# Loading the first image ahead of the small weights, touching two activation tables early, and spare matrix products at two places of a convolution-attention-recurrence kernel

## The chip, the cores and the metric

The kernel runs on one core of a Trainium2 chip. The metric is device time in microseconds: the median of three runs of the kernel before is 6977.31 us (6975.09 to 6978.62).

## What is computed

The input x has four images of 128 channels by 64 x 64 points, in float32. Each image goes through two layers, and the second ends in a recurrence that runs over all four together. Cut to what matters:

```
# layer 0: attention over 4096 points, after a normalisation over groups of 4 channels
xn    = (x - mean_g) / sqrt(var_g + 1e-5)             # needs the whole image first
e1,e2 = prelu(w1 @ xn + b1, a1), prelu(w2 @ xn + b2, a2)
asm   = prelu(wa @ xn + ba, aa)
x     = x + softmax(e1^T e2) applied to asm
# layer 1, per token (t = x transposed)
t = t + attention(layer_norm(t))                      # 16 heads of 8, queries = cos products;
                                                      # inside: zf = cos(.) * cos(ry); h = relu(zf @ w1.T + b1)
t = t + rnn(layer_norm(t)):                           # Wx = layer_norm(t) @ W.T, batch norm over all tokens
    y_t = sigmoid(Wx_t + y_{t-1} @ V.T)               # 4096 steps
```

## The kernel before, in words

**The order of the work.** The body first loads the weights and prepares them, then goes through the four images in a loop. For each image `first_stage` runs layer 0 (and, beside it, the feed-forward part of the image before), and `second_stage` runs the attention of layer 1. After the loop `last_stage` does the feed-forward part of the fourth image, and a last part (the stage named "runs") does the recurrence and writes the output. In these stages the order of TensorE's, ScalarE's and VectorE's instructions is written by hand: what stands earlier in the code is earlier in the engine's queue, and an engine whose next instruction waits does nothing behind it. The queues of SP and, outside the attention, of GpSimd are filled by a scheduler which knows only dependencies and the order of the code.

**The head.** The weights of layer 0 (w1, w2, b1, b2, wa, aa, a1, a2) are loaded by GpSimd (L152, L139, L162), all other weights by ScalarE's queue (L139, L200 to L207), and the first image by SP in four pieces of 512 KB (L1512). VectorE negates a1/a2, aa and b1/b2 (L167, L169), splits the rows of biases into a rounded part and a rest (L326 to L328), takes the statistics of the image in eight pieces of 512 columns (`norm_stats`: `bn_stats` at L350, the aggregate at L353, then two small products on TensorE at L357 and L366 that sum over channel groups, with the small operations L359 to L363 and L239 and a power on GpSimd at L241 between and after them). It also takes the cosine of `ry` (L246 to L253, the sine table on ScalarE at L255), scales a weight matrix by it, splits it (L317 to L320) and lets SP copy half of the rest part (L322). These preparing tiles lie in a pool named setup, which is closed before the images begin; its memory is used again by the image's tile q.

**Layer 0.** `layer0` begins with `first_pieces`: VectorE normalises 512 columns into q (L378), TensorE makes the convolutions (L391, L427, with the bias rows as a product with ones at L296), ScalarE applies the two halves of prelu (L398, L399, L337, L338), VectorE joins them (L410, L339) and splits e2 and e1 into rounded part and rest (L414, L415, L484, L485). Then for 8 blocks of 512 queries and 16 pairs of key tiles: two products per tile on TensorE (L503), exp on ScalarE (L507), the weighted sum on TensorE (L514), and the running total on VectorE (L528). Within each block `meanwhile` is called 16 times; it advances by one step the work per token of the block before (`tokens`: transposes, layer norm, cosines). A float32 product appears in the profile as two MATMUL instructions.

**The recurrence.** 4096 steps are run as 128 runs of 32 steps beside each other, each with 14 steps ahead of it from a guessed state (`WARM`), in two halves k of the images. Eight PSUM banks are first written by a product (L1790), then VectorE writes into each bank the scaled inputs of two steps (`seed`, L1808), TensorE adds the product with V (L1837), and ScalarE applies the sigmoid (L1842). From step 10 on VectorE also adds the results to the rows t2 (L1821), which are then stored (L1857). The last lines compare two states and decide on a slow exact way, which is not taken here.

Of the kernel before, what the change touches and what calls it, by code (L numbers as in the profile page):

```python
# [10 lines left out]
F32 = mybir.dt.float32  # L11
# [15 lines left out]
def kernel(  # L27
# [107 lines left out]
    loader = [nc.gpsimd]  # L135
# [9 lines left out]
    def load_both(one, two, name, axis):  # L145

        shape = list(one.shape)
        shape[axis] *= 2
        t = const.tile(shape, F32, tag=name, name=name)
        for i, ap in enumerate((one, two)):  # L150
            part = t[:, ts(i, CR)] if axis else t[ts(i, CR), :]
            nc.gpsimd.dma_start(out=part, in_=ap)  # L152
        return t
# [7 lines left out]
    for i, ap in enumerate((a1, a2)):  # L161
        nc.gpsimd.dma_start(out=a12_sb[ts(i, CR), :], in_=ap.partition_broadcast(CR))  # L162
# [3 lines left out]
    for t in (a12_sb, aa_sb):  # L166
        nc.vector.tensor_scalar(t, t, -1.0, None, ALU.mult)  # L167
    minus_b12 = const.tile([P, 1], F32, tag="minus_b12", name="minus_b12")
    nc.vector.tensor_scalar(minus_b12, b12_sb, -1.0, None, ALU.mult)  # L169
# [3 lines left out]
    for sign, base in ((1, 0), (-1, 3)):  # L173
# [10 lines left out]
    loader[0] = nc.scalar  # L184
    rx_bc = load_row(rx, "rx_bc")
    wc_sb = load(w_combT, "wc_sb")

    f1_sb = const.tile([P, NF, P], F32, tag="f1_sb", name="f1_sb")
    ry_sb = once.tile([P, 1], F32, tag="ry_sb", name="ry_sb")
    nc.gpsimd.memset(ry_sb, 0.0)  # L190
    setup = ctx.enter_context(ExitStack())
    setup_pool = setup.enter_context(tc.tile_pool(name="setup", bufs=1, reuse_waits="tile"))
    f1_all, f1_low = (
        setup_pool.tile([P, NF * P], F32, tag=name, name=name) for name in ("f1_all", "f1_low")
    )
    biases = setup_pool.tile([33, 4, P], F32, tag="biases", name="biases")
    nc.gpsimd.memset(f1_all, 0.0)
    for i in range(2):
        for k, ap in enumerate((ba, b_comb, fb2, be1)):
            nc.scalar.dma_start(out=biases[ds(32 * i, 1), k, :], in_=ap)  # L200
    for g in range(4):
        nc.scalar.dma_start(out=f1_all[ds(D * g, D), :], in_=f1T)
        nc.scalar.dma_start(out=ry_sb[ds(D * g, D), :], in_=ry)
    fb1_sb, f2_sb = load(fb1, "fb1_sb"), load(f2T, "f2_sb")
    g1_bc, be1_z = load_row(g1, "g1_bc"), const.tile([P, D], F32, tag="be1_z", name="be1_z")
    be1_bc = setup_pool.tile([P, P], F32, tag="be1_bc", name="be1_bc")
    nc.scalar.dma_start(out=be1_bc, in_=be1.partition_broadcast(P))  # L207
    g2_bc, be2_bc = load_row(g2, "g2_bc"), load_row(be2, "be2_bc")
    WT_sb, VT_sb = load(WT, "WT_sb"), load(VT, "VT_sb")
    gamma_sb, beta_sb = load(gamma, "gamma_sb"), load(beta, "beta_sb")  # L210


    nc.vector.tensor_copy(be1_z, be1_bc[:, 0:D])
# [98 lines left out]
    ck = once.tile([P, 1], F32, tag="ck", name="ck")  # L312
    cr = once.tile([P, 1], F32, tag="cr", name="cr")
    cry = once.tile([P, 1], F32, tag="cry", name="cry")
    for _ in cos_steps(cry, ry_sb, ck, cr):
        pass
    nc.vector.tensor_scalar(f1_all, f1_all, cry, None, ALU.mult)  # L317
    f1_high = f1_sb.rearrange("p f e -> p (f e)")
    nc.vector.tensor_copy(f1_high.bitcast(F32R), f1_all)
    nc.vector.tensor_tensor(f1_low, f1_all, f1_high, ALU.subtract)  # L320

    nc.sync.dma_start(out=f1_high[ds(2 * D, 2 * D), :], in_=f1_low[ds(2 * D, 2 * D), :])  # L322

    for row in (0, 32):
        at = slice(row, row + 1)
        nc.vector.tensor_tensor(biases[at, 2], biases[at, 2], biases[at, 3], ALU.add)  # L326
        nc.vector.tensor_copy(bias_rows[at].bitcast(F32R), biases[at, 0:3])
    nc.vector.tensor_tensor(  # L328
        bias_rows[at].bitcast(F32R), biases[at, 0:3], bias_rows[at], ALU.subtract
    )  # L330
    setup.close()


# [1174 lines left out]
    def load_x(n, rows):  # L1508

        xs = by_channel.tile([P, S], F32, tag="xs", name=f"xs{n}")  # L1510
        for i in range(4):
            nc.sync.dma_start(out=xs[:, ts(i, S // 4)], in_=x_rows[rows, ts(i, S // 4)])  # L1512
        return xs

# [54 lines left out]
    def first_stage(im, before):  # L1569
# [12 lines left out]
        with stage(f"conv{n}", {}, others, **pools, **psum), tc.manual_schedule(engines=engines):  # L1582
            own, calls = [], [0]
            step_late = in_steps(feed_forwards(before) if before else [], 13, 3)

            def meanwhile(steps=1):

                calls[0] += 1
                if before and calls[0] in (14, 17, 20):
                    before["left"].pop(0)()  # L1590
                for _ in range(steps):
                    step_first(own)

                for _ in range(0 if calls[0] <= 8 else 2 if calls[0] % 8 == 0 else 1):
                    step_late()

            norm = im["norm"] or list(norm_stats(n, im["xs"]))[-1]
# [129 lines left out]
    x_rows = x.rearrange("n c s -> (n c) s")  # L1727
    t2_rows = [t2_dram[ts(n, P), :] for n in range(N)]
    before = None
    x_next = {"xs": load_x(0, ts(0, P))}  # L1730
# [9 lines left out]
    for n in range(N):  # L1740
        image = open_image(n, ts(n, P), "right" if n % 2 else "left", **x_next)
        tail = first_stage(image, before)
# [22 lines left out]
    with stage("runs", t2=((P, 2 * IC), 4 * N), half=(HALF, 2 * NS + 2), ps_one=(ONE, NS * NB)):  # L1765
# [22 lines left out]
        for j in range(NB):  # L1788
            for k in range(NS):
# [7 lines left out]
                )  # L1797

# [27 lines left out]
        with tc.manual_schedule(  # L1826
            engines={nc.tensor.engine, nc.scalar.engine, nc.vector.engine}
        ):
            y = [None] * NS
# [164 lines left out]
```

## Time and profile before

| | us |
|---|---|
| median of three runs | 6977.31 |
| profiled execution, its own time | 6976.16 |
| its span in the trace | 6974.4 |
| first normalisation of the first image (L378) begins | 23.86 |
| first exp of layer 0 (L507) begins | 35.74 |
| first sigmoid (L1842) begins | 6884.95 |
| last instruction of VectorE (L1877) begins | 6960.72 |

The page of the profile gives, first, each engine's busy time. A view of groups gives, for a kind of instruction, how many there are, their mean time and what ended the idle time before them. The timeline gives instructions of one kind that follow each other as one line: start and length in us from the start of the span, engine, line of the code, operation, tile written and tiles read, shapes, how many, and in square brackets how long the engine stood idle before and for whom. ACTq and SPq are the queues in which ScalarE and SP issue DMAs; the length there is that of the issue, not of the transfer.

### The profile page before, as it was taken

The page shows a single profiled execution, that of the slowest core. Times are in us where ns is not written, and L with a number is a line of the kernel's source. Part 1 is how long each engine was busy: PE and PEld are TensorE (multiplying, and loading weights), DVE is VectorE, ACT ScalarE, POOL GpSimd, SP SyncE. Part 2 cuts the span into 40 slices and gives each one's busy share as a digit, 9 for nine tenths or more (in the row PEclk, how much of TensorE's full clock was granted, in tenths as well). Part 3 has the DMA queues.
Part 4 walks back from the last instruction along what each step waited for, and adds up shares of the span by engine and source line. Part 5 has one row for each costly group of instructions (what it writes and reads, how often), then busy time and mean ns, then how long its engine had stood idle before and what let it go on. Part 6 is the DMA issues. An engine that isn't in the chain of part 4 may idle for free. (4 is left out here: it accounts for less than half of the span.)

```text
span 6974.4 us, 223486 instructions
## 1 busy us (share of the span) xinstructions
PE 6808.2 (98%) x92333; PEld 3655.8 (52%) x92333; DVE 5966.9 (86%) x8064; ACT 5937.1 (85%) x11843; POOL 2795.6 (40%) x10008
## 2 busy tenths in 40 slices
PE   8999999999999999999999999999999999999997
PEld 4545555555664555555565455555456555555554
DVE  6688889897888898888787989898978898988887
ACT  4479999996669999999565999999956699999985
POOL 1134444444333444443433344444343344444442
PEclk9999999999999999999999999999999999999998
DMA  1110000000111000000011100000001100000012
GB/s 32 37 41 25 24 28 21 22 10 23 46 51 42 28 21 22 21 22 9 31 49 52 37 22 21 22 21 24 22 22 50 52 30 22 21 25 24 19 62 110
DMA packets 84760, 219.87 MB, mean 32 GB/s; under 512 B 9384, under 2 KB 10288, under 8 KB 82960
## 3 DMA queue, kind: packets, MB, share of 16 engines
q1 hardware_dynamic: 80448, 200.34, 8.5%
q8 instruction: 726, 11.89, 0.7%
q10 hardware_dynamic: 3024, 4.99, 0.2%
q14 instruction: 306, 2.51, 0.1%
q0 software_dynamic: 256, 0.13, 0.0%
HBM read 141.44 MB, written 56.62 MB: 28 GB/s over the span
## 5 line engine op out<-in xcount | busy, mean ns | idle before, releaser
L1069 ACT ACTIVATE e<-s 128x1024 f32<-128x1024 f32 (+1 forms) x3480 | 2952.7, 903 | 113.1 <-PE s L1057 82.8
L832 DVE STREAM_TRANSPOSE t<-e 128x1024 f32<-128x1024 f32 x2240 | 2594.0, 1210 | 75.7 <-ACT e L1069 73.0
L845 PEld LDWEIGHTS misc<-t,mirror 128*32 128x32 f32 x57344 | 1655.4, 110 | 1327.5 <-issue 1270.4
L845 PE MATMUL misc<-t,mirror 128*32 128x128 f32 x57344 | 1967.1, 273 | 18.7 <-DVE later L859 15.9
L1069 ACT ACTIVATE xs<-s 128x1024 f32<-128x1024 f32 (+1 forms) x2152 | 1840.7, 910 | 54.4 <-PE s L1057 42.6
L832 DVE STREAM_TRANSPOSE t<-xs 128x1024 f32<-128x1024 f32 x1344 | 1562.5, 1210 | 42.8 <-ACT xs L1069 41.3
L866 PE MATMUL acc<-e,q_aug 128*32 128x512 f32 x11360 | 1523.4, 608 | 1.1 <-POOL q_aug L748 1.1
L1057 PE MATMUL s<-queries,keys 32*128 32x512 f32 x9216 | 1245.9, 496 | 20.1 <-ACT e L1069 10.0
L912 POOL COPY own<-o 32x36 f32<-32x36 f32 x2048 | 430.4, 210 | 1802.5 <-DVE o L904 1722.6
L514 PE MATMUL acc<-p,asmT 128*128 128x512 f32 x2048 | 947.7, 594 | 1.6 <-DVE e L410 1.6
L866 PE MATMUL acc<-xs,q_aug 128*32 128x512 f32 x7072 | 942.2, 605 | 0.0
L507 ACT ACTIVATE p<-s 128x1024 f32<-128x1024 f32 x512 | 500.2, 1023 | 404.7 <-PE s L503 400.7
L1057 PEld LDWEIGHTS s<-queries,keys 32*128 32x128 f32 x9216 | 487.9, 182 | 602.1 <-issue 297.2
L937 POOL COPY other<-turned 32x64 f32<-32x64 f32 x1904 | 449.5, 236 | 622.4 <-DVE turned L927 543.9
L1069 ACT ACTIVATION_READ_ACCUMULATOR e<-s 128x1 f32 x2880 | 697.0, 242 | 0.0
L802 POOL COPY mirror<-q 32x128 f32<-32x128 f32 x2048 | 604.3, 295 | 198.5 <-PE misc L845 110.7
L503 PE MATMUL s<-hl,e 128*128 128x512 f32 x2048 | 587.7, 428 | 21.0 <-ACT hl L465 11.1
L528 DVE TENSOR_TENSOR total<-total,p 128x1024 f32<-128x1024 f32 x448 | 547.6, 1222 | 22.0 <-ACT p L507 14.3
L514 PEld LDWEIGHTS acc<-p,asmT 128*128 128x128 f32 x2048 | 380.4, 190 | 335.6 <-issue 310.9
L503 PEld LDWEIGHTS s<-hl,e 128*128 128x128 f32 x2048 | 380.4, 189 | 177.7 <-issue 68.6
L1069 ACT ACTIVATION_READ_ACCUMULATOR xs<-s 128x1 f32 x1728 | 422.4, 244 | 0.0
L898 POOL COPY by_token<-by_key 32x4 f32<-32x4 f32 x2000 | 385.8, 193 | 84.5
(314 smaller groups left out, 4434.4 us busy)
## 6 DMA issues: line engine op xcount, KB each, us to landing
keys<-parts_dram SPq DMA_DIRECT2D x256, 256.0 KB
queries<-parts_dram SPq DMA_DIRECT2D x1024, 32.0 KB
x_dram<-x SPq DMA_DIRECT2D x56, 256.0 KB
fx<-x_dram SPq DMA_DIRECT2D x48, 256.0 KB
xs<-in_x_dram SPq DMA_DIRECT2D x16, 512.0 KB
t_dram<-t2T SPq DMA_DIRECT2D x32, 256.0 KB
t2s<-t_dram SPq DMA_DIRECT2D x16, 512.0 KB
hl<-hl SPq DMA_DIRECT2D x28, 256.0 KB
```

What stands on the lines that cost most here:

```text
L503: nc.tensor.matmul(s[:, j, :], stationary, moving, start=y == 0, stop=y == len(parts) - 1)
L507: nc.scalar.activation(p, s, AF.Exp)
L514: nc.tensor.matmul(state["acc", ic], asmT[:, ts(2 * jp + j, P)], p[:, j, :], start=jp == 0 and j == 0, stop=jp == NP - 1 and j == 1,)
L528: nc.vector.tensor_tensor(state[ic], state[ic], p, ALU.add)
L802: nc.gpsimd.tensor_copy(wv[ts(a, 32), s, :, :, ts(a, D)], own[ts(s, 32)])
L832: nc.vector.transpose(group["e"][h][:, k, :], es[h])
L845: nc.tensor.matmul(state["acc"][ts(2 * x + h, 32), :], state["w"][:, QT * (s // 4) + TG * x + s % 4, h, :], state["e"][h][:, :, ds(IC * x ...
L866: nc.tensor.matmul(it["in"]["acc"][ts(2 * h + x, 32), :], it["qa"][:, ds((2 * it["tiles"][x] + h) * V, 32)], it["e"][h][:, ts(x, IC)], sta ...
L912: nc.gpsimd.tensor_copy(own[ts(s, 32), ts(x, 4), h, :], ov[ts(2 * h + x, 32), s, :, 0:V])
L937: copy(to[ts(k, 32), h], tv[ts(2 * x + h, 32), k])
L1057: nc.tensor.matmul(ss[h][:, x, :], keys[unit[x] // QT].bitcast(F32R)[r, ts(unit[x] % QT, P)], queries[b].bitcast(F32R)[r, :], start=True, ...
L1069: nc.scalar.activation(es[h][:, ts(x, IC)] if split else es[h], ss[h][:, x, :] if split else ss[h].rearrange("p x c -> p (x c)"), AF.Exp, ...
```

## The change

There are five edits.

1. The first image is loaded by the first DMAs of the program, in eight pieces of 256 KB, alternately from SP's and ScalarE's queue. The other images are loaded as before.
2. The weights of layer 0 are loaded by ScalarE's queue behind that instead of by GpSimd, and most other weights by SP's queue. `first_weights` holds what VectorE does with the weights of layer 0: the row ba is loaded twice into a piece of q, the negations stand behind the aggregate of the statistics, the split of the bias row behind the operation that makes tv (L363).
3. The preparation of the other weights becomes `other_weights`, a generator that `meanwhile` advances in the first image's layer 0 at its calls 6 (all loads), 26 (the cosine), 29 (scaling and splitting) and 32 (bias rows and SP's copy). Its tiles come from a pool of that stage; the pool named setup is gone.
4. ScalarE runs an exp on a 128 x 1 tile at the first image's beginning, and a sigmoid on it ahead of the recurrence's first seed.
5. TensorE gets three products of ones with the first three pieces of x behind the first `bn_stats`, into a bank that nobody reads, and four more products into the last two of the recurrence's eight banks, behind the eight that were there.

The diff, cut to its core:

```diff
-    loader = [nc.gpsimd]
+    x_rows = x.rearrange("n c s -> (n c) s")
+
+    def load_x(n, rows, engines=(nc.sync,), pieces=4):
+
+        xs = by_channel.tile([P, S], F32, tag="xs", name=f"xs{n}")
+        for i in range(pieces):
+            part = ts(i, S // pieces)
+            engines[i % len(engines)].dma_start(out=xs[:, part], in_=x_rows[rows, part])
+        return xs
+
+    x_next = {"xs": load_x(0, ts(0, P), (nc.sync, nc.scalar), NIC)}
+    loader = [nc.scalar]
...
-            nc.gpsimd.dma_start(out=part, in_=ap)
+            loader[0].dma_start(out=part, in_=ap)
...
-        nc.gpsimd.dma_start(out=a12_sb[ts(i, CR), :], in_=ap.partition_broadcast(CR))
+        nc.scalar.dma_start(out=a12_sb[ts(i, CR), :], in_=ap.partition_broadcast(CR))
...
+    def first_weights(room):
+
+        for row in (0, 32):
+            nc.scalar.dma_start(out=room[row : row + 1, :], in_=ba)
+        yield
+
+        for t in (a12_sb, aa_sb):
+            nc.vector.tensor_scalar(t, t, -1.0, None, ALU.mult)
+        nc.vector.tensor_scalar(minus_b12, b12_sb, -1.0, None, ALU.mult)
+        yield
+        for row in (0, 32):
+            at = slice(row, row + 1)
+            nc.vector.tensor_copy(bias_rows[at, 0].bitcast(F32R), room[at, :])
+        nc.vector.tensor_tensor(
+            bias_rows[at, 0].bitcast(F32R), room[at, :], bias_rows[at, 0], ALU.subtract
+        )
+        yield
+
+    def other_weights():
...
+        nc.gpsimd.memset(f1_all, 0.0)
+        nc.gpsimd.memset(ry_sb, 0.0)
+        for i in range(2):
+            for k, ap in enumerate((b_comb, fb2, be1)):
+                nc.sync.dma_start(out=biases[ds(32 * i, 1), k, :], in_=ap)
+        for g in range(4):
+            nc.sync.dma_start(out=f1_all[ds(D * g, D), :], in_=f1T)
+            nc.sync.dma_start(out=ry_sb[ds(D * g, D), :], in_=ry)
+        nc.sync.dma_start(out=be1_bc, in_=be1.partition_broadcast(P))
+        yield
+
+        nc.vector.tensor_copy(be1_z, be1_bc[:, 0:D])
+        cr, cry = (once.tile([P, 1], F32, tag=name, name=name) for name in ("cr", "cry"))
+        for _ in cos_steps(cry, ry_sb, ck, cr):
+            pass
+        yield
+        nc.vector.tensor_scalar(f1_all, f1_all, cry, None, ALU.mult)
+        f1_high = f1_sb.rearrange("p f e -> p (f e)")
+        nc.vector.tensor_copy(f1_high.bitcast(F32R), f1_all)
+        nc.vector.tensor_tensor(f1_low, f1_all, f1_high, ALU.subtract)
+        yield
+
+        nc.sync.dma_start(out=f1_high[ds(2 * D, 2 * D), :], in_=f1_low[ds(2 * D, 2 * D), :])
...
             def meanwhile(steps=1):
 
                 calls[0] += 1
+                if n == 0 and calls[0] in (6, 26, 29, 32):
+                    next(weights, None)
...
-            norm = im["norm"] or list(norm_stats(n, im["xs"]))[-1]
+            norm = im["norm"]
+            if norm is None:
+                signs = im.get("signs", iter(()))
+                for i, norm in enumerate(norm_stats(n, im["xs"])):
+                    if n == 0 and i == 0:
+                        warm = one_psum("warm_conv")
+                        for k in range(3):
+                            nc.tensor.matmul(
+                                warm, ones, im["xs"][:, ts(k, IC)], start=True, stop=True
+                            )
+                    if i >= NIC:
+                        next(signs, None)
...
-    x_next = {"xs": load_x(0, ts(0, P))}
+    loader[0] = nc.sync
+    rx_bc = load_row(rx, "rx_bc")
+    wc_sb = load(w_combT, "wc_sb")
...
+    fb1_sb, f2_sb = load(fb1, "fb1_sb"), load(f2T, "f2_sb")
+    g1_bc, g2_bc, be2_bc = load_row(g1, "g1_bc"), load_row(g2, "g2_bc"), load_row(be2, "be2_bc")
+    WT_sb, VT_sb = load(WT, "WT_sb"), load(VT, "VT_sb")
+    gamma_sb, beta_sb = load(gamma, "gamma_sb"), load(beta, "beta_sb")
...
         image = open_image(n, ts(n, P), "right" if n % 2 else "left", **x_next)
+        if n == 0:
+            image["signs"] = first_weights(image["q"][:, S - P : S])
+            next(image["signs"])
+            nc.scalar.activation(ck, half_pi, AF.Exp)
...
+        for _ in range(2):
+            for k in range(NS):
+                nc.tensor.matmul(
+                    banks[k][NB - 1],
+                    ones.bitcast(F32R),
+                    bias_rows[:, 0, :].bitcast(F32R).unsqueeze(1).broadcast_to([P, TG, P]),
+                    start=True,
+                    stop=True,
+                    skip_group_check=True,
+                )
...
+            nc.scalar.activation(ck, half_pi, AF.Sigmoid)
             y = [None] * NS
```

More of the change, by code (lines that the diff above doesn't have):

```diff
@@ L161 @@
     for i, ap in enumerate((a1, a2)):
-        nc.gpsimd.dma_start(out=a12_sb[ts(i, CR), :], in_=ap.partition_broadcast(CR))
+        nc.scalar.dma_start(out=a12_sb[ts(i, CR), :], in_=ap.partition_broadcast(CR))
     bias_rows = const.tile([P, 3, P], F32, tag="bias_rows", name="bias_rows")
     nc.gpsimd.memset(bias_rows, 0.0)
-    for t in (a12_sb, aa_sb):
-        nc.vector.tensor_scalar(t, t, -1.0, None, ALU.mult)
     minus_b12 = const.tile([P, 1], F32, tag="minus_b12", name="minus_b12")
-    nc.vector.tensor_scalar(minus_b12, b12_sb, -1.0, None, ALU.mult)
     grp = const.tile([P, P // 4, 4], F32, tag="grp", name="grp")
@@ L183 @@
     grp = grp.rearrange("p a b -> p (a b)")
[L184 to L213, printed above, removed]
     ident = const.tile([P, P], F32, tag="ident", name="ident")
@@ L309, in row4 @@
         return bc.unsqueeze(1).broadcast_to([P, TG, P])
[L312 to L331, printed above, removed]
+    def first_weights(room):
[13 more added lines that the diff above has]
+        yield
@@ new lines, in other_weights @@
+    def other_weights():
+        f1_all, f1_low, rows, row = (
+            get("fhalf", name) for name in ("f1_all", "f1_low", "bias_parts", "be1_row")
+        )
+        biases = rows[0:33].rearrange("p (k e) -> p k e", e=P)
+        be1_bc = row[:, 0:P]
+        nc.gpsimd.memset(f1_all, 0.0)
[19 more added lines that the diff above has]
+        nc.sync.dma_start(out=f1_high[ds(2 * D, 2 * D), :], in_=f1_low[ds(2 * D, 2 * D), :])
+        for row in (0, 32):
+            at = slice(row, row + 1)
+            nc.vector.tensor_tensor(biases[at, 1], biases[at, 1], biases[at, 2], ALU.add)
+            nc.vector.tensor_copy(bias_rows[at, 1:3].bitcast(F32R), biases[at, 0:2])
+        nc.vector.tensor_tensor(
+            bias_rows[at, 1:3].bitcast(F32R), biases[at, 0:2], bias_rows[at, 1:3], ALU.subtract
+        )
@@ L1506, in fold_norm @@
         nc.vector.tensor_copy(WsT, pw[:, 0:P])
[L1508 to L1513, printed above, removed]
     def open_image(n, rows, side, xs, norm=None):
@@ L1582, in first_stage @@
         with stage(f"conv{n}", {}, others, **pools, **psum), tc.manual_schedule(engines=engines):
-            own, calls = [], [0]
+            own, calls, weights = [], [0], other_weights()
             step_late = in_steps(feed_forwards(before) if before else [], 13, 3)
@@ L1595, in meanwhile @@
                     step_late()
-            norm = im["norm"] or list(norm_stats(n, im["xs"]))[-1]
+            norm = im["norm"]
[7 more added lines that the diff above has]
+                                warm, ones, im["xs"][:, ts(k, IC)], start=True, stop=True
+                            )
+                    if i >= NIC:
+                        next(signs, None)
             layer0(
@@ L1725, in last_stage @@
                 tick += 1
-    x_rows = x.rearrange("n c s -> (n c) s")
     t2_rows = [t2_dram[ts(n, P), :] for n in range(N)]
     before = None
-    x_next = {"xs": load_x(0, ts(0, P))}
+    loader[0] = nc.sync
+    rx_bc = load_row(rx, "rx_bc")
+    wc_sb = load(w_combT, "wc_sb")
+    f1_sb = const.tile([P, NF, P], F32, tag="f1_sb", name="f1_sb")
+    ry_sb, ck = (once.tile([P, 1], F32, tag=name, name=name) for name in ("ry_sb", "ck"))
+    be1_z = const.tile([P, D], F32, tag="be1_z", name="be1_z")
+    fb1_sb, f2_sb = load(fb1, "fb1_sb"), load(f2T, "f2_sb")
+    g1_bc, g2_bc, be2_bc = load_row(g1, "g1_bc"), load_row(g2, "g2_bc"), load_row(be2, "be2_bc")
+    WT_sb, VT_sb = load(WT, "WT_sb"), load(VT, "VT_sb")
+    gamma_sb, beta_sb = load(gamma, "gamma_sb"), load(beta, "beta_sb")
     def prepare_image(n):
@@ L1797 @@
                 )
+        for _ in range(2):
[7 more added lines that the diff above has]
+                    skip_group_check=True,
+                )
         def sums_at(k, t):
```

## Prediction

> **What bounds the kernel now.** I read the page first, then the timeline of VectorE, of the two DMA queues and of ScalarE in the first 40 us, then the recurrence. The page says where a gain can't come from:
>
> ```profile
> span 6974.4 us, 223486 instructions
> PE 6808.2 (98%) x92333; PEld 3655.8 (52%) x92333; DVE 5966.9 (86%) x8064; ACT 5937.1 (85%) x11843; POOL 2795.6 (40%) x10008
> ```
>
> TensorE is busy 98% of the span, and the change takes away none of the products in between. Only the two ends count, where TensorE waits. At the head VectorE's timeline carries the order of things:
>
> ```profile
> 5.68 0.69 DVE L350 BATCH_NORM_STATS2 gst<-xs 128x6 f32<-128x512 f32 x1 [4.40 <-DMA xs<-in_x_dram]
> 8.43 0.15 DVE L169 TENSOR_SCALAR minus_b<-b_sb 128x1 f32<-128x1 f32 x1 [2.06 <-DMA b_sb<-in_b_dram]
> ...
> 15.12 0.69 DVE L350 BATCH_NORM_STATS2 gst<-xs 128x6 f32<-128x512 f32 x1
> 15.85 0.37 DVE L353 BATCH_NORM_AGGREGATE gmv<-gst 128x2 f32<-128x48 f32 x1
> 16.95 0.16 DVE L359 COPY gm<-pg 128x1 f32<-128x1 f32 x1 [0.74 <-PE pg L357]
> ...
> 18.24 0.16 DVE L239 TENSOR_SCALAR v_g<-pv 128x1 f32<-128x1 f32 x1 [0.68 <-PE pv L366]
> ...
> 23.86 1.00 DVE L378 TENSOR_SCALAR q<-xs,gm,r_g 128x512 f32<-128x512 f32 x2 [2.16 <-DMA f_sb<-f_low]
> ```
>
> The statistics end at 15.81 although eight of them are 5.5 us of work: they wait for x and for small weights queued between them. GpSimd's power ends at 19.06, yet the normalisation starts at 23.86, because the cosine, the scaling and the copy of f_low stand before it, and q lies in the memory of the setup pool. Why x is late, the two DMA queues show:
>
> ```profile
> 2.99 0.27 ACTq L200 DMA_DIRECT2D biases<-in_be_dram  x1
> 5.67 1.89 SPq L1512 DMA_DIRECT2D xs<-in_x_dram  x2
> 5.86 0.23 ACTq L200 DMA_DIRECT2D biases<-in_ba_dram  x1
> ```
>
> Up to 2.99 eight transfers were issued (six by ScalarE's queue, two pieces of x). The ninth goes out only at 5.67, when the first piece of x has landed (L350 starts at 5.68). So both queues share eight places, taken in turn. At the end and after the first scores ScalarE shows:
>
> ```profile
> 34.44 1.28 ACT L507 ACT_TABLE_LOAD   x1
> 35.74 1.94 ACT L507 ACTIVATE p<-s 128x1024 f32<-128x1024 f32 x2
> ...
> 6883.66 1.28 ACT L1842 ACT_TABLE_LOAD   x1 [2.48 <-DVE wx L1808]
> 6884.95 0.66 ACT L1842 ACTIVATE warm<-wx 128x256 f32<-128x256 f32 x2
> 6886.14 0.39 ACT L1842 ACTIVATE warm<-wx 128x256 f32<-128x256 f32 x1 [0.53 <-PE wx L1837]
> ```
>
> Both table loads stand on the path. The granted clock there, from the view of stretches (the columns after the length are busy times; then clock, DMA share, GB/s):
>
> ```profile
> 6883.80:6886.00 2.20, 0.61 (x3) 0.56 (x4) 2.20 (x4) 1.80 (x3) 0.00 (x0) 0.99 1.04 389
> 6886.00:6889.40 3.40, 3.40 (x10) 2.02 (x9) 3.40 (x6) 1.54 (x4) 0.00 (x0) 0.51 0.99 370
> 6889.40:6892.80 3.40, 3.28 (x13) 1.66 (x13) 2.58 (x4) 2.31 (x6) 0.00 (x0) 1.00 1.03 412
> ```
>
> A stretch with TensorE mostly idle is followed by 3.4 us at half clock.
>
> **What the Trainium skill says.** "DMA: Bandwidth & Descriptors", Issuing engines are not separate DMA queues: two issuing queues share the same 16 engines and save issue time only. The trace agrees so far: the second image's load, from SP alone, moves 344 to 393 GB/s. So x comes early by being first and by holding all eight places, not by the second queue. "TensorE: Matmul & The Clock Gate", Part 1: the clock is halved after an idle window and given back after a busy one of about 3.4 us, with windows that run free of the program; the 0.99, 0.51, 1.00 above agree. "ScalarE: Activation LUTs", What ACT_TABLE_LOAD costs: 1283 ns and a drain of some 1380 ns. The load agrees (1.28); the drain doesn't show (34.44 to 35.74), so I use 1.3.
>
> **The head, step by step.** *x.* In the second image's load the stretches from 1617 hold 53, 287, 344, 393, 385, 344, 350 KB per us: 2097 KB are through 7.1 us after the issue at 1616.76. Here the issue is at 0.83; with half a us until the landing is seen, the last pair of pieces is there at L = 8.4, with one late engine 9; I take 8.8. The statistics keep up with the pairs (two take 1.4, a pair comes every 1.4), so they end at 8.8 + 1.4 = 10.2 and the aggregate at 10.6, against 16.22.
>
> *The chain behind it* is unchanged: from 15.81 to 19.15 it was 3.35 us. With nothing in the way q would start at 10.2 + 3.35 = 13.5.
>
> *What stands in the way now.* VectorE's negations (three of 0.12 to 0.15) stand behind the aggregate, the bias row's split (three, estimated at 0.7 from 0.26 to 0.35 for those of L326 and L327) behind tv. Their work fits into the waits of 0.74 and 0.68 for pg and pv, so it costs nothing. But each waits for its weights, and all else on VectorE waits behind it: gm, tv, v_g, then everything. ScalarE's queue issues the eight weights and ba twice behind its four pieces of x, and each needs a place. If SP's eleven loads take places in turn with them, as x did with ScalarE's loads before, only four of the ten go out for pieces of x; the last of these, b2, goes out at 8.9, when x6/x7 land; a2 waits for b2's place (or for f2T, 256 KB), ba' for aa's. A landing costs 2.0 us at the least (f_low: issued at 21.73, q free at 23.8) and 5.2 at the most (b_sb, in the DMA view of before); in a mostly empty queue I take 2.3. So b2 lands at 11.3, a2 goes out at 11.4 and lands at 13.7; negations to 14.2; gm to tv takes 0.6; ba' lands at about 14.5; v_g at 15.6; power and normalisation start 0.9 later: **q at 16.5**, a gain of 23.86 - 16.5 = **7.4 us**. If the scheduler puts all ten ahead of SP's, a2 waits only for x7: lands 11.4, and q starts at 14.2, gain 9.7.
>
> *Exp table.* ScalarE loads it while it has nothing else to do (before 28.28 it waited 8.34 us). At 34.44 it is gone; the scores were there at 34.9 less the same shift, the first weighting needs p. Gain **1.3**. GpSimd's loads, 0.55 to 1.07 each, were beside the path: 0.
>
> *Products of ones.* Six MATMULs at 0.85 cold (as L391 at 25.48 to 27.18) from about 4.5 last until 9.6, before pg at 10.7: cost 0. Until the first convolution at 17 TensorE is then idle but for pg and pv (0.56 each): by the windows above it is cold again. Gain 0; if it stayed warm, four products of 0.85 would take 0.43: 2.
>
> **The moved work.** Call 6 puts fifteen DMAs on SP: with x off it, SP has nothing to do from 10 us until the copy of hl at 66.49, so the cover is tens of us. Call 26 adds seven operations of about 0.19 to VectorE (1.3 us) at about 117, and to ScalarE a sine table, 0.29 and the exp table again (2.9 us). ScalarE stands idle 3.32 us before the exp at 122.43, but the exp table is loaded only when the scores are there (127.74, 1.33 idle before it), so p is 1.3 late; it is used 5 us later. Calls 29 and 32 add 1.6 and about 2 us to VectorE, which waits 3.92 us for ScalarE at 126.44 and 2.24 at 136.63. TensorE waits for nobody between 100 and 345 us. Cost 0; without cover it would be 2.9 + 4.9, and I keep 0 to 1 as the range: **-0.3**.
>
> **The end.** The sigmoid on ck goes into ScalarE's gap from 6881.2 to 6883.66. Then the first half's sigmoid starts at 6883.66 instead of 6884.95, the second's when its seed is done (6884.3) instead of 6885.23: the pair gains 0.9. The half-clock stretch goes if TensorE stays busy: four more products take 0.9 to 1.7 and end between 6883.7 and 6884.5, the first product of the recurrence is due at 6884.1, so they delay it by 0.4 at most. Before, the fourth pair of sigmoids ended its ramp at 6889.56 with a pace of 1.17 from there on; at full pace from 6884.95 it would be at 6888.46: 1.1. Sum 0.9 + 1.1 = 2.0, range 0.5 to 2.4. VectorE's adds from 6914.88 to 6956 run without a gap, so the whole rest moves by the same: **2.0**.
>
> **Sum.** 7.4 + 1.3 - 0.3 + 2.0 = 10.4 us. The profiled execution took 6976.16 (span 6974.4, 1.8 around it), 1.1 below the median; the difference goes from the median: 6977.3 - 10.4 = **6966.9 us**, -0.15%. About 0.2%, 14 us, is what a measurement of this kernel can tell from no change.
>
> **The rivals.**
> - *Weights in time.* All ten loads stand directly behind x. For it: they come earlier in the code than SP's. Against: x, late in the code, still went out at 0.83, as its queue was free. 9.7 + 1.3 + 2.0 = 13.0: 6964.3.
> - *And warm.* The same with the first convolutions at full clock, by the products of ones or a luckier window: 15: 6962.3. Against: 4 us of near idleness.
> - *Eaten up.* Moved work disturbs layer 0, or the window falls badly at 17 us (3.4 us more at half clock): 5: 6972.3.
> - *Slower: the last small weight comes later than before.* Place: VectorE's negations and bias split, behind ScalarE's queue. Price: 5.2 us per round of places, if landings are as slow as GpSimd's were. Four rounds behind L: 8.8 + 20.8 = 29.6, plus 1.6 to q: 31.2, 7.3 later than before, less 3.3: +4, 6981. It decides from q at 27.2, that is from ba' landing after 25.6. Against: queues are nearly empty after x.
> - That the change doesn't do what it says can be only in the products of ones (above).
>
> **How the numbers follow.** Forecast 0.38, weights in time 0.30, and warm 0.15, eaten up 0.09, slower 0.08. Of these, faster by over 14 us are nearly all of the warm case, 0.13 of weights in time and 0.03 of the forecast: 0.30. Slower by over 14 us: 0.03, the far end of the last. The rest, 0.67, is within 0.2%. The range, 6960 to 6974.5, holds all but the slower case, half of the eaten-up one and the ends of the others; the forecast's own is 6964 to 6970.
>
> **What would show it.** Right: eight issues of x by 2.6; last L350 ending at 10 to 11; idle time of VectorE before L167's operations "<-DMA a_sb", q at 16 to 17; first exp without a table load; sigmoids from 6884.95 minus the shift at a pace of 1.17 with clock 1.00. Wrong: x landing after 10, q before 15 or after 18, new waits of TensorE between 100 and 345, a shift between 345 and 6870 that grows or shrinks with the images.

## The result and the profile after

The changed kernel took 6966.07 us (median of 22 runs, 6959.67 to 6969.24) beside 6975.71 us (22 runs, 6973.71 to 6980.50) of the kernel before: 9.6 us less, ratio 0.9984, 95% interval 0.9978 to 0.9991, that is 6 to 15 us. The profiled execution took 6959.67 us, the lowest of the 22. Its span is 16.4 us shorter than that of the profiled execution before, so most of what lies between 9.6 and 16.4 must be a property of the two executions and not of the kernels. The page's first lines:

```profile
span 6958.0 us, 223501 instructions
PE 6809.2 (98%) x92343; PEld 3655.4 (53%) x92343; DVE 5967.9 (86%) x8067; ACT 5939.8 (85%) x11847; POOL 2784.3 (40%) x10000
```

TensorE's busy time is what it was (6808.2); what went away is waiting at the two ends. VectorE's timeline of the head:

```profile
4.57 3.82 DVE L365 BATCH_NORM_STATS2 gst<-xs 128x6 f32<-128x512 f32 x6 [3.31 <-DMA xs<-in_x_dram]
8.64 1.29 DVE L365 BATCH_NORM_STATS2 gst<-xs 128x6 f32<-128x512 f32 x2 [0.25 <-DMA xs<-in_x_dram]
9.96 0.37 DVE L368 BATCH_NORM_AGGREGATE gmv<-gst 128x2 f32<-128x48 f32 x1
15.03 0.15 DVE L297 TENSOR_SCALAR a_sb<-a_sb 128x1 f32<-128x1 f32 x1 [4.70 <-DMA a_sb<-in_a_dram]
...
17.38 1.00 DVE L393 TENSOR_SCALAR q<-xs,gm,r_g 128x512 f32<-128x512 f32 x2 [0.69 <-POOL r_g L219]
```

The statistics end at 9.93 instead of 15.81. Then VectorE stands 4.70 us before a negation of one column, because the slopes a_sb have not landed, and gm, whose sum TensorE had ready at 11, stands behind it. Why, ScalarE's timeline with its queue shows:

```profile
7.70 1.63 ACTq L163 DMA_DIRECT2D b_sb<-in_b_dram  x2
9.37 0.60 ACTq L150 DMA_DIRECT2D wa_sb<-in_waT_dram  x1
10.00 0.45 ACTq L150 DMA_DIRECT2D aa_sb<-in_aa_dram  x1
10.49 1.39 ACTq L173 DMA_DIRECT2D a_sb<-in_a_dram  x2
13.84 0.76 ACTq L293 DMA_DIRECT2D q<-in_ba_dram  x2
14.62 1.28 ACT L1774 ACT_TABLE_LOAD   x1 [14.62 <-DMA a_sb<-in_a_dram]
...
106.06 1.28 ACT L1872 ACT_TABLE_LOAD   x1
107.40 0.20 ACT L1872 ACTIVATE ck<-half_pi 128x1 f32<-128x1 f32 x1
107.62 1.28 ACT L233 ACT_TABLE_LOAD   x1
108.92 0.30 ACT L233 ACTIVATE cry<-cr,half_pi 128x1 f32<-128x1 f32 x1
109.34 1.28 ACT L522 ACT_TABLE_LOAD   x1
...
6870.94 1.28 ACT L1886 ACT_TABLE_LOAD   x1 [2.51 <-DVE wx L1851]
6872.23 0.66 ACT L1886 ACTIVATE warm<-wx 128x256 f32<-128x256 f32 x2
6873.40 0.88 ACT L1886 ACTIVATE warm<-wx 128x256 f32<-128x256 f32 x2 [0.51 <-PE wx L1881]
```

The second slope (the later of the two issues in the line of a_sb) goes out at 11.41 and is there at 15.0, 3.6 us later. And the early sigmoid (L1872) is not where the source has it: it runs at 107.40, in the first layer, between two exps, and the table load stands on the path at 6870.94 as before. The first exp, at 27.88, has no table load in front of it. Set against the first profiled execution of before, instruction by instruction, the changed kernel is 6.48 us ahead at 20 to 30 us and 7.87 from 40 to 400. This lead, by how much earlier the same instruction starts, is used below. Between 500 and 6800 us it wanders (8.4, 9.6, 9.3, 10.8, 10.3, 11.9, 11.1), and it stands at 13.7 at VectorE's end.

### The profile page after: what moved, and what is told of

Read it like the earlier page. It is cut to its first block, busy times and chain, and to the rows that moved or that the text cites. A ratio compares the mean times of both kernels' runs of the same rounds, so it can differ in the third digit from the quotient of the medians.

```text
span 6958.0 us, 223501 instructions
## 1 busy us (share of the span) xinstructions
PE 6809.2 (98%) x92343; PEld 3655.4 (53%) x92343; DVE 5967.9 (86%) x8067; ACT 5939.8 (85%) x11847; POOL 2784.3 (40%) x10000
## 5 line engine op out<-in xcount | busy, mean ns | idle before, releaser
L518 PE MATMUL s<-hl,e 128*128 128x512 f32 x2048 | 585.8, 427 | 22.6 <-ACT hl L480 11.2
```

The lines of the kernel that those rows point to most:

```text
L518: nc.tensor.matmul(s[:, j, :], stationary, moving, start=y == 0, stop=y == len(parts) - 1)
```

## The experiments

**A second trace of each kernel.** The wandering lead might come from the moved work or from the clock's windows, the stretches of 3.4 us in which TensorE's granted clock stays the same.

> The changed kernel once more, for a second trace. My theory: the change moves the head (the first normalisation at 17.4 us, the first exp at 27.9, so 7.9 us earlier than before at 40 to 400 us) and the start of the recurrence (pace of 1.17 from the first pair of sigmoids, 1.1 us); everything else in the first trace's 16.4 us is the place of the clock's windows. Then this trace has the same 7.9 at 40 to 400, and other steps at the image boundaries, off by 1 us or more from those of the first trace (1.7 more at 1650 to 3370, 2.9 more at 3400 to 3800, 4.0 more at 5200 to 5500, 5.9 more at 6890). Rival: these steps belong to the moved work; then they come back within 0.3 us. Time: 6966, 3 either way.

> The kernel before once more, for a second trace of it. Against the one trace of before, four of five traces of the changed kernels gain 1.2 at 1643 us, 1.5 at 3360 and some 1 at 5080, where the first trace of before had windows at half clock (1643 and 1667, 3353 and 3370, 5080) that the others had not. Luck theory: this trace has another set of half-clock windows there, and its times at 1700, 3450 and 5200 differ from the first trace's by 1 us or more. Rival (the windows stand firm against the program, and the shift of the head decides which pieces of work they halve): the same set, times within 0.3 us of the first trace's up to 6800.

The changed kernel again: 6964.92 us (21 runs; before 6977.00, 54 runs; ratio 0.9983, 0.9977 to 0.9990). Its lead was 6.55 and 7.93, and the later steps did come back within 0.4 us up to 6860, which spoke for the rival. But they had all been counted from one trace of before, and the second trace of before settled it: one run, 6971.39, span 6969.7, was 0.24 behind the first trace at 40 to 400 us, 1.7 ahead at 1800, 3.1 at 3500, 2.2 at 5400 and 5.4 at 6900. The stretches at half clock at 1643, 1667 and 3353 us were not there. So steps of this size come without the edit, with the half-clock stretches, and two traces of one kernel can lie 4.7 us apart. The last step of the changed kernel's lead, from 10.8 to 13.8 between 6860 and 6890, is mostly of this kind too: some 1.9 of it lie ahead of the last statistics, where the first trace of before ran at half clock for 20.5 us from 6862 on and the second for 6.8 us from 6859 on; only 1.1 lies at the sigmoids. From here on only stretches are compared, not spans.

**What holds the small weights up.** Three kernels that differ from the changed one in its loads. The first was to issue the larger loads later:

> The changed kernel with the eleven larger loads of the sync queue (rx to beta) issued after the statistics, at the sixth call of the convolutions, ahead of the bias rows and f1. The ten small weights then have the queues and the memory to themselves behind x. Theory that those loads hold the small weights up (places in turn, or the bytes they move): the second slope a lands at 11.2 to 12.4 instead of 15.0, the first normalisation starts at 13.2 to 15.0 instead of 17.4, 14.2 is my value; the kernel is 2.4 to 4.2 us faster than the changed one: about 6963. Rival, that the landing of a 256-byte transfer is slow by itself (3.5 us) or that the scalar queue is what takes the time: the normalisation at 16.5 to 17.5 and no gain. Second rival: the eleven loads come too late for their users or disturb the first layer: new waits of TensorE between 27 and 345 us, a loss of 1 to 5.

```python
+            later.append((t, ap))
...
+        for t, ap in later:
+            nc.sync.dma_start(out=t, in_=ap)
```

The first line stands in load, for the loads of the sync queue, the others in other_weights, at the sixth call. The edit did not do what it was for. In the trace the eleven loads go out from 4.57 on, as before the edit, since nothing they depend on is late; the scheduler moved them up. Normalisation at 17.67, 6963.46 us: it tells nothing on the question.

> The changed kernel with the same eleven loads issued by GpSimd instead of the sync queue: they move the same bytes at the same early time, but through a queue that took no part in the two queues' taking of places in turn before. Places theory: the scalar queue then issues its ten right behind x, the normalisation starts at 13.5 to 15. Bandwidth theory (the 860 KB of these loads keep the engines busy and the small ones wait in line): a_sb still lands at about 15 and the normalisation starts at 16.5 to 17.5, or later, as the loads now come between the pieces of x and the statistics end after 10.5. Rival: GpSimd issues slowly, its power for the normalisation (r_g) stands behind the eleven issues and the normalisation waits for that, at 16 or later.

```python
-    loader[0] = nc.sync
+    loader[0] = nc.gpsimd
```

The numbers are those of the bandwidth theory: a_sb landed at 15.4, the statistics ended at 11.24 and the normalisation started at 17.83 (6965.90 us). GpSimd's own work was not what it waited for: VectorE waited 0.70 us for r_g, as in the changed kernel (0.69). (The eleven loads are 647 KB in the DMA view, not 860.) But the run doesn't separate the two theories cleanly. The scalar queue still waited for pieces of x, which came later here (wa went out at 8.97), so the second slope was issued at 11.05, little earlier than before, and then took 4.3 us to land while GpSimd's transfers moved. So places in turn are not all of it.

> What the run with late loads was meant to be: the eleven larger loads of the sync queue now follow a one-element copy of the normalisation's scale into each tile, so they can't go out before the first normalisation; the ten small weights have queues, places and engines to themselves behind x. Theory that those loads hold the small weights up: the scalar queue issues without the turns (second slope a by about 9.5 instead of 11.5), it lands by 12, the first normalisation starts at 13.3 to 14.5 instead of 17.4, and the shift at 40 to 400 us grows from 7.9 to about 11. Rival: the landing of such transfers (64 or 128 packets of 4 bytes each) is slow by itself, some 3.5 us from issue, as in the run with GpSimd's loads (issued at 11.66, landed 15.4): then at best the issue comes earlier, the normalisation at 15 to 16. Second rival: the loads now come too late for the first tokens, and TensorE gets new waits between 60 and 345 us.

```python
+            corner = t[:, 0, 0:1] if len(t.shape) == 3 else t[:, 0:1]
+            nc.gpsimd.tensor_copy(corner, normed[0])
             nc.sync.dma_start(out=t, in_=ap)
```

Here normed[0] is the scale r_g of the normalisation. ScalarE's queue in this kernel, then VectorE's timeline:

```profile
7.72 0.33 ACTq L153 DMA_DIRECT2D wa_sb<-in_waT_dram  x1
8.10 0.44 ACTq L153 DMA_DIRECT2D aa_sb<-in_aa_dram  x1
9.02 1.12 ACTq L176 DMA_DIRECT2D a_sb<-in_a_dram  x2
```

```profile
12.03 0.15 DVE L300 TENSOR_SCALAR a_sb<-a_sb 128x1 f32<-128x1 f32 x1 [1.48 <-DMA a_sb<-in_a_dram]
...
14.40 1.00 DVE L400 TENSOR_SCALAR q<-xs,gm,r_g 128x512 f32<-128x512 f32 x2 [0.68 <-POOL r_g L222]
```

With the larger loads out of the way the second slope goes out 1.9 us earlier (9.53) and lands 1.1 us faster (2.5 instead of 3.6). The normalisation starts at 14.40, 3.0 earlier. Both halves of the first theory hold: the larger loads cost the small ones places and also time to land. At 40 to 400 us the lead was 9.9, not the 11.2 by which the first exp was ahead (24.54 instead of 35.74): TensorE's clock was halved once more from 24.7 to 28.1, in the first scores. It is 9.9 at 40 to 60 and at 300 to 400 us alike, so the late loads held nobody up. Time 6962.49 (20 runs; ratio 0.9980, 0.9974 to 0.9987).

> The changed kernel with one part of the change undone: the eight small weights (w1 to a2) are issued by GpSimd again, ahead of its masks, as in the kernel before; only ba, twice, stays on the scalar queue behind x. In the kernel before they landed by 9.4 us. Theory that the small weights' place behind x is what costs the head 3 to 4 us of its possible gain: a_sb lands by 10, the statistics end at 10 to 11 (up to 1 us later, as the small packets move among x), ba lands by 12, the normalisation starts at 13.3 to 14.5, 3 to 4 us earlier than in the changed kernel. Rival: x is held up as much as the weights gain, the statistics end at 12 or later and the normalisation at 15.5 or later. Rival: ba is the next late thing, at 14 or later.

```python
-    loader = [nc.scalar]
+    loader = [nc.gpsimd]
...
-        nc.scalar.dma_start(out=a12_sb[ts(i, CR), :], in_=ap.partition_broadcast(CR))
+        nc.gpsimd.dma_start(out=a12_sb[ts(i, CR), :], in_=ap.partition_broadcast(CR))
```

```profile
9.40 1.29 DVE L365 BATCH_NORM_STATS2 gst<-xs 128x6 f32<-128x512 f32 x2 [0.47 <-DMA xs<-in_x_dram]
10.72 0.37 DVE L368 BATCH_NORM_AGGREGATE gmv<-gst 128x2 f32<-128x48 f32 x1
11.01 0.10 DVE L297 TENSOR_SCALAR a_sb<-a_sb 128x1 f32<-128x1 f32 x1
...
11.68 0.16 DVE L374 COPY gm<-pg 128x1 f32<-128x1 f32 x1 [0.45 <-PE pg L372]
...
13.87 1.00 DVE L393 TENSOR_SCALAR q<-xs,gm,r_g 128x512 f32<-128x512 f32 x2 [0.70 <-POOL r_g L219]
```

The negation no longer waits; x pays 0.8 us for it (the statistics end at 10.69), and the normalisation starts at 13.87, 3.5 earlier than in the changed kernel, as the first theory had it. The lead at 40 to 400 us is 11.4. Time 6963.19 (17 runs; ratio 0.9982, 0.9975 to 0.9990): the medians say 2 to 3 us, which these intervals can't tell from the changed kernel; the trace can.

**The early sigmoid and the spare products.**

> The changed kernel with the early sigmoid made to read the mean of the products' statistics (its result is used by nobody), so that it can't be moved ahead to the first layer and stands in ScalarE's gap before the first seed. Theory: the table load runs at about 1.5 us before the first seed is done, the first pair of sigmoids starts 1.3 us earlier after the last statistics (4.3 instead of 5.6 us), the second of the pair 0.9 earlier because its seed is then the last to come; the end comes 0.9 us earlier: too little for the times, read from the trace. Rival: the load is hidden behind the seeds or spare products anyway, so the fourth pair of sigmoids stands where it stood (9.1 us after the start of the last statistics): 0. In the first layer the pair of table loads at 106 to 108 us is gone, which changes nothing (0 at 120 to 345).

```python
+        held["bmv"] = bmv[:, 0:1]
...
-            nc.scalar.activation(ck, half_pi, AF.Sigmoid)
+            nc.scalar.activation(ck, held["bmv"], AF.Sigmoid)
```

The first line stands behind the aggregate of the products' statistics. ScalarE's timeline:

```profile
6867.09 1.02 ACT L1492 COPY every<-pwx 128x512 f32<-128x512 f32 x1 [1.95 <-DVE wx_stats L1490]
6868.12 1.28 ACT L1873 ACT_TABLE_LOAD   x1
6869.42 0.20 ACT L1873 ACTIVATE ck<-bmv 128x1 f32<-128x1 f32 x1
6870.64 0.39 ACT L1887 ACTIVATE warm<-wx 128x256 f32<-128x256 f32 x1 [1.02 <-issue]
6871.36 0.83 ACT L1887 ACTIVATE warm<-wx 128x256 f32<-128x256 f32 x2 [0.34 <-DVE wx L1852]
```

Now the load lies in ScalarE's gap. The first sigmoid starts 4.28 us after the start of the last statistics instead of 5.56, the second when its seed is done, the fourth pair (a pair is one sigmoid of each half) at 7.84 instead of 9.08 or 10.13. Time 6963.02 (11 runs; ratio 0.9979, 0.9970 to 0.9988).

> The changed kernel without the four spare products in front of the recurrence. In four traces with them and the table load where it was, the fourth pair of sigmoids came 9.08 us after the start of the last statistics twice and 10.13 twice (10.16 in the trace of before). Theory: the spare products save the window only when it falls rightly; without them 10.1 to 10.2 again. Rival: the window's place alone decides, and 9.1 can be had without them. Elsewhere no difference: 7.9 us ahead of before at 40 to 400 us.

Without the four products (the loop `for _ in range(2)` taken out) the fourth pair stood at 10.13, as in both traces of before. With them, and the table load in its old place, it stood at 9.1 in three traces of seven (the first of the changed kernel, and the runs with late and with held loads) and at 9.8 to 10.1 in four. Time 6966.14 (21 runs; ratio 0.9985, 0.9979 to 0.9992). At 40 to 400 us the lead was 7.3 instead of 7.9, since the normalisation started at 17.90; the head is the same code, so it varies by half a us from trace to trace. What decides at the recurrence is one window of the clock, in which TensorE has nothing but those products between the last product for the statistics and the first of the recurrence. From the view of stretches, without the products, with them in the second trace of the changed kernel, with them in the first, and with the true early sigmoid:

```profile
6873.70:6877.20 3.50, 0.50 (x3) 0.06 (x1) 2.87 (x7) 1.50 (x2) 0.34 (x1) 1.00 0.94 366
6877.20:6880.60 3.40, 3.18 (x7) 2.19 (x8) 3.40 (x6) 1.42 (x5) 0.00 (x0) 0.50 0.98 342
```

```profile
6868.80:6872.20 3.40, 1.30 (x6) 0.72 (x4) 2.90 (x7) 1.53 (x2) 0.20 (x1) 1.00 1.01 347
6872.20:6875.60 3.40, 3.21 (x8) 2.18 (x8) 3.40 (x6) 1.43 (x5) 0.00 (x0) 0.50 0.91 286
```

```profile
6868.80:6872.20 3.40, 1.58 (x7) 0.94 (x5) 2.62 (x6) 1.26 (x1) 0.48 (x1) 1.00 0.93 343
6872.20:6875.60 3.40, 2.89 (x11) 1.67 (x11) 3.40 (x6) 2.22 (x7) 0.00 (x0) 1.00 0.93 310
```

```profile
6868.70:6872.10 3.40, 2.36 (x9) 1.35 (x8) 2.84 (x7) 1.97 (x5) 0.27 (x1) 1.00 0.98 372
6872.10:6875.50 3.40, 3.23 (x13) 1.65 (x12) 3.40 (x6) 2.15 (x7) 0.00 (x0) 1.00 0.95 340
```

The first number after the length is TensorE's busy time, the third from the end the clock. With 0.50 or 1.30 us busy the next window runs at half clock, with 1.58 or 2.36 at full. The four products put the window just at the edge; the earlier first sigmoid shortens the gap itself and clears it (in all three traces of kernels that have it). Without either, the fourth pair stood at 10.1 to 10.2 in all four traces (this one, both of before, and the last run below). Four against three of seven are too few to exclude chance; the busy times are what speaks for the products.

**The products of ones at the head.**

> The changed kernel without the three products of ones on x. In its traces they make TensorE's clock full from 8.0 to 11.4 us, and it is halved again from 11.4 to 21.6, before the first convolution at 18. Theory: they are worth 0: without them the clock stays halved from the start until a window after the convolution, its four passes of pc take 3.77 us again, the first exp comes at 27.9 and the shift at 40 to 400 us is 7.9 (within 0.4 for the landing of the weights). Rival: they help by the place of the next full window, and without them the clock comes back one window (3.4 us) later: 1 to 2 us lost at 40 to 400.

One run, 6968.35 us. The normalisation started at 17.71 (a_sb landed 0.3 later, within what the head varies by) and the first exp at 27.80 instead of 27.88, so they bring nothing up to there. Then a window from 28.0 to 31.4 ran at half clock, and the lead at 40 to 400 us was 6.7 instead of 7.9. The same happened at 24.7 in the kernel with held loads, which has the products. One trace can't say whether their absence caused it.

**Both gains together, and a warm TensorE.**

> The changed kernel with the eight small weights issued by GpSimd again and the early sigmoid reading the mean of the products' statistics: the two parts that gained by themselves. Theory, both gains stand on the path at the two ends and add: first normalisation at 13.9, 11.4 us ahead of the first trace of before at 40 to 400; first pair of sigmoids 4.3 us after the start of the last statistics, the fourth at 7.8; together 3.5 + 1.2 (to 2.3 where the window had been lost) = 4.7 to 5.8 better than the changed kernel's 6965.5: about 6960. Rival: the clock's windows take back part of the head's gain in the first layer, as in the run with held loads (9.9 instead of 11.3 at 40 to 400), or the fourth pair stands at 9 again, because the window is lost without the half-clock's cause having gone: 6962 to 6964.

6960.24 us (14 runs, before 6975.28; ratio 0.9981, 0.9973 to 0.9989). The lead was 11.2 at 40 to 400 us, the sigmoids stood at 4.28 and the fourth pair at 7.84: both gains are there. It is the lowest median of the study, 4.7 to 5.8 us below the two of the changed kernel; the intervals of the two ratios overlap.

> The kernel of the run with both parts, with the products of ones carried on to the first convolution: on all eight pieces of x as they land, two ahead of the first group's sum pg, one between pg and pv, four between pv and pc. TensorE then is never idle for more than about half a window between 4.5 and 14.5 us. Theory: the clock stays full from 8 on, pc's four passes take 1.9 instead of 3.8, the bias product 0.5 instead of 0.85 to 1.27, the first exp comes 1.5 to 2.5 us earlier than without (24.4), and all after it: about 6958. Rival: pg and pv stand behind spare products and come up to 0.5 late each, the normalisation moves to 14.5 or later, and the scores wait for VectorE and ScalarE, which a faster TensorE doesn't help: 0 or a loss of up to 1. Second rival: the window before the convolution still counts as idle (two thirds at most busy), pc stays at 3.8.

6963.83 us (21 runs; ratio 0.9984, 0.9977 to 0.9991), a loss beside the last, by the rival's first mechanism and much larger than it said. TensorE's timeline:

```profile
4.73 10.27 PE L1615 MATMUL warm_conv<-xs,ones 128*128 128x512 f32 x20 [4.73 <-DMA xs<-in_x_dram]
14.84 0.28 PE L372 MATMUL pg<-gmv,grp 128*128 128x1 f32 x2
...
16.06 3.68 PE L1615 MATMUL warm_conv<-xs,ones 128*128 128x512 f32 x8
19.58 1.88 PE L406 MATMUL pc<-q,w_sb 128*128 128x512 f32 x4
```

I had sized the spare work wrongly: each product is two records, the first ten keep TensorE busy until 14.8, and pg, which ran at 11.46 in the kernel without, stands behind them (normalisation at 17.34 instead of 14.03). What a warm first convolution is worth can still be worked out. pc's four records take 1.88 us; in the run with both gains it was 3.78:

```profile
14.63 3.78 PE L406 MATMUL pc<-q,w_sb 128*128 128x512 f32 x4 [1.54 <-DVE q L393]
```

From the start of the normalisation to the first exp it is 10.24 us against 10.52, only 0.3 less. But pc starts 2.24 us after the normalisation here and 0.60 there, because the last four spare products stand ahead of it until 19.58: they take back 1.6 of the 1.9. From pc's end to the first exp it is 6.1 us in both. So a warm pc that started in time would bring the first exp some 1.9 us forward; that is an estimate from these two traces, no run shows it. Three other traces speak for it: where the full clock came back during pc (without the products of ones, with held loads, with the true sigmoid), pc took 3.37, 3.41 and 3.71 us instead of 3.78, and the first exp came 10.09, 10.13 and 10.43 us after the normalisation instead of 10.50.

**The tail.** From VectorE's last cast (bad_int) to the end of the span it was 13.5 and 14.2 us in the traces of before, and 10.8 to 11.9 in all of the changed kernels.

> The kernel before, with its branch of recovery, which is not taken, made longer by 24 instructions of the sync queue (its loads of t2 in four parts each); nothing that runs is changed. In both traces of before the sync queue stands still for 2.3 and 2.7 us behind its eighth instruction after the end of that branch, with an instruction fetch in the gap, and the span ends 13.5 and 14.2 us after VectorE's last cast; in no trace of the changed kernels is there such a gap (10.8 to 11.9 us). Theory: the queue's code crosses a fetch boundary there, and the change's 30 more instructions on it moved the boundary away, by accident. Then here the gap is gone, the span ends 10.8 to 11.9 us after the cast, and the time is 2.5 us below that of before (6973). Rival: the gap belongs to the kernel before's queues (GpSimd's transfers, twelve waits at the end instead of eight) or to chance; then it is there again, 13.5 or more.

```python
-                    nc.sync.dma_start(out=t2s[:, n, :], in_=t2_rows[n][:, ds(s0, SC)])
+                    for j in range(4):
+                        part = SC // 4
+                        nc.sync.dma_start(
+                            out=t2s[:, n, ts(j, part)], in_=t2_rows[n][:, ds(s0 + j * part, part)]
+                        )
```

VectorE's last row in the kernel before, in the changed one, and in this one, each with the line of its span:

```profile
core 0 of [0], span 6974.4 us
...
6960.72 0.14 DVE L1877 CAST bad_int<-bad 1x1 int32<-1x1 f32 x1
```

```profile
core 0 of [0], span 6958.0 us
...
6947.02 0.14 DVE L1921 CAST bad_int<-bad 1x1 int32<-1x1 f32 x1
```

```profile
core 0 of [0], span 6969.1 us
...
6957.81 0.14 DVE L1877 CAST bad_int<-bad 1x1 int32<-1x1 f32 x1
```

From the cast's end that is 13.5, 10.8 and 11.2 us. The sync queue's instructions at the end of the branch (L1883) and at the end of the program, in the kernel before and in this one, with the start of the first and of the last:

```profile
L1883 SPq EVENT_SEMAPHORE  x8: 17/17/17, 6969.8 to 6970.4; - x8
L1990 SPq EVENT_SEMAPHORE  x14: 17/28/28, 6972.7 to 6974.3; - x14
```

```profile
L1883 SPq EVENT_SEMAPHORE  x8: 17/17/17, 6966.9 to 6967.4; - x8
L1994 SPq EVENT_SEMAPHORE  x14: 17/28/28, 6967.5 to 6969.1; - x14
```

The gap behind the eighth instruction (6970.4 to 6972.7) is gone in the second. The time, 6972.44 us (13 runs, before 6975.07; ratio 0.9996, 0.9988 to 1.0005), agrees with 2.5 without showing it. Code that never runs moved the end, and the queues of this kernel are those of before, so the changed kernel most likely owes some 2.5 us to the length of its code.

## Why the prediction was right, and where it was not

The total was close, 6966.9 against 6966.07, but that is in part luck: the head and the sigmoid fell short by 0.9 us each, and 2.5 us at the tail, which the prediction did not have, made up for them.

| step | predicted | traces show |
|---|---|---|
| head, to the normalisation | 7.4 | 6.5 |
| exp table | 1.3 | 1.4 |
| products of ones | 0 | 0 (or a window later) |
| moved work | -0.3 | 0 |
| sigmoid table | 0.9 | 0 |
| clock at the recurrence | 1.1 | 1.1 or 0 (two traces) |
| tail | - | 2.5 |
| sum | 10.4 | 10.4 to 11.5 |

- **x and the statistics** were right: the last pair was there at 8.64 (8.8 predicted), the statistics ended at 9.93 (10.2), the aggregate at 10.33 (10.6).
- **Places in turn** were right: SP's loads went out between ScalarE's, and the second slope went out at 11.41 (11.4). The mis-sized term is the landing: "in a mostly empty queue I take 2.3". The engines were not empty, the larger loads were landing too, and it took 3.6, where with those held back it took 2.5. The Trainium skill's "DMA: Bandwidth & Descriptors", Latency and other measured facts, has a possible reason: the fixed cost of a transfer is mostly the round trip to memory, and it is smaller when the load on that memory is lighter. No run here separates that from waiting behind the larger loads' packets on the engines. So the slopes came 1.3 late; the chain behind them was 0.4 faster than I had it, which leaves the 0.9 between 16.5 and 17.4. The 5.2 that the prediction calls the most a landing takes is that of b_sb; the two loads of w_sb took 5.6 and 6.2 in the same view.
- **The exp table** and the drain that didn't show: 7.87 - 6.48 = 1.39. Again the trace shows no drain of the kind that the Trainium skill's "ScalarE: Activation LUTs", What ACT_TABLE_LOAD costs, has beside the load: 14.62 + 1.28, then ck at 15.92.
- **The moved work** cost nothing: the lead is 7.87 at 40 to 60 and at 300 to 400 us, with three table loads in between at 106 to 110.
- **The sigmoid** is the step whose mechanism failed: "The sigmoid on ck goes into ScalarE's gap from 6881.2 to 6883.66". The sentence "That the change doesn't do what it says can be only in the products of ones" ruled out what happened: the sigmoid ran at 107.40, and its table load stayed on the path at 6870.94. The instruction reads a constant and writes a dead column; nothing tied it to its place. Tied to a late value, it gained 1.2 by the sigmoids' places.
- **The clock** fits in mechanism, and its size is a matter of odds: about 1 in three traces of seven, 0 to 0.4 in four. The Trainium skill's "TensorE: Matmul & The Clock Gate", Part 1, says that the windows run free and a kernel differs from run to run by their phase; the pairs of traces here agree (the fourth pair of sigmoids at 9.08 and 10.13 in the two of the changed kernel).
- **If it stayed warm: 2** was about right in size: pc is 1.9 shorter at full clock, and what comes behind it takes as long as before. The three products of ones don't bring it, as the prediction says, and the one run that kept TensorE warm lost it by its own spare products.
- **The tail** wasn't in the sum at all. Without it the sum by the traces would be 7.9 to 9.0. The measured 9.6 and 12.1 (6977.00 - 6964.92) hold either, since each comparison's interval is some 9 us wide; the tail rests on traces, two with the gap and twelve without.
- **A sign of being wrong came**, a lead that changes from image to image. The second trace of before shows steps of the same size without the edit, so it doesn't speak against the prediction.

What stays open: how much busy time in a window keeps the clock. 1.30, 1.31 and 1.40 us of 3.4 were followed by half clock at the recurrence, 1.42, 1.58 and 1.72 were not. But 1.54 was, in the run without the products of ones, and so were 1.66 and 1.69 in the first layer. The profile's busy time alone doesn't decide it. Whether the steps of the lead at the image boundaries have a mean other than 0 would take many traces.

## What to carry to other kernels

When a load is moved ahead of others, follow the last small transfer behind it: here a column of slopes took back 3.5 us of what x had gained, and issuing it early cost x only 0.8. A prefetch of a table holds only if its instruction reads something late; look in the trace for where it really ran. With effects of 1 us in 7000, take two traces of each kernel and compare stretches of work, and count the code's length and the clock's windows among the causes.

## What the runs showed of the hardware

- The sync queue stood still for 2.3 to 2.7 us behind the end of a branch that is jumped over; 24 instructions more in the branch, never run, took that away. A piece of code that has to be fetched is the likely cause, not a shown one: fetches of instructions lie in the gap, and one more follows it than in the other kernels.
- A column of 64 values of 4 bytes landed 2.5 us after its issue with the engines nearly idle, 3.6 to 4.3 beside loads of 64 to 256 KB.
- What the clock takes from or gives to the first convolution reaches the first exp in full: pc shorter by 0.41, 0.37 and 0.07 us in three traces, the first exp earlier by 0.41, 0.37 and 0.07 us, counted from the start of the normalisation.
- Two executions of one kernel, same code, had their half-clock windows at different image boundaries, and lay up to 3.6 us apart in mid-course and 5.4 near the end.
